# A selective-scan stack: VectorE takes delta*x for its own products from SBUF, without ScalarE's copy into PSUM

## The chip, the core and the metric

The kernel runs on one NeuronCore of a Trainium2 chip. The metric is the device time of one execution in microseconds (us), the median of several runs; before the change it is 22066.67 us, over three runs of 22064.29 to 22081.29 us. The core has a matrix engine (TensorE, PE in the profile), a vector engine (VectorE, DVE), an activation engine (ScalarE, ACT), a general engine (GpSimd, POOL) and an engine that issues the transfers (SyncE, SP). Each of them takes its own instructions in order. They wait for each other through semaphores. Two on-chip memories matter here: SBUF, the large one, and PSUM, the small one that TensorE writes its results into.

## What is computed

Four layers run over an input of 4 images, 64 x 64 positions, 128 channels. Layers 0, 1 and 3 are state-space blocks: normalisation, projection, a 3 x 3 convolution, four selective scans (by rows, by columns, and both of these backwards), a gate and a small network. Layer 2 is a gating layer. The scans are most of the work; cut to what matters:

```python
delta = softplus(dts + dt_b)
A = -exp(A_log).reshape(K, DI, N)                 # K = 4 scans, DI = 256 channels, N = 16 states

def step(h, t):
    x_t, d_t, B_t, C_t = t
    h = exp(d_t[..., None] * A) * h + (d_t * x_t)[..., None] * B_t[:, :, None, :]
    return h, einsum('bkdn,bkn->bkd', h, C_t)     # y: the sum over the 16 states
```

For each channel and each of 16 states this is a recurrence along 4096 positions with a decay `exp(delta*A)` and an input `(delta*x)*B`. `B` and `C` depend on the position and the state and not on the channel.

## The kernel before

The 4096 positions are cut into chunks of 512 (`CH`). A chunk belongs to one image, one layer and one of the four scans; there are 384 of them (12 turns of image and layer, 4 scans, 8 chunks). The 256 channels lie in two halves `m` of 128 partitions, the 16 states in four groups `q` of 4. A chunk is worked in 8 periods (`i`), one for each pair of group and half, so there are 3072 periods. Each period handles 4 states of 128 channels over 512 positions, in two sides of two states each:

- Side 0: the input is made by TensorE. `pair_db` multiplies the transposed delta*x with diagonal matrices of B (which ScalarE made in `diagonals`, line 891) into the PSUM tile `dbp` (line 899).
- Side 1: the input is made by VectorE. ScalarE's `lift` (line 916) copies one half of `s.du`, the product delta*x, from SBUF into a PSUM tile `dv`, at the end of the period before. Two products (lines 1048 and 1049) multiply it by the rows of B in `s.bb`. The first writes the other of two `dv` tiles, the second writes over its own input. Both have 128 x 512 elements, one operand in PSUM (`dv`) and one in SBUF (`bb`).

For each of the four states, ScalarE makes the decay `da` (line 908), VectorE runs the recurrence (`scan`, line 924) from `da` in SBUF and `dbp` or `dv` in PSUM into `h` in SBUF, and ScalarE saves the last element as the next chunk's initial state (`save`, line 932). GpSimd multiplies both states of a side by the rows of C, `cb` (`times_c`, line 936, 128 x 1024 elements), and in every second period adds the two sides (line 938). TensorE sums over the states by matmuls with the identity (line 951), and VectorE takes the sum out of PSUM (lines 962 and 964). GpSimd also makes `s.du` from delta and x, once per half and chunk (line 859). SyncE loads `bb` and `cb` as rows that are broadcast over the partitions (line 875).

The order on each engine is the order of the calls in the loop over `periods` (lines 985 to 1071); the program is scheduled by hand. In one period VectorE has: scan, scan (side 0), product, product, scan, scan (side 1). Everything else (normalisations, projections, convolutions, the small networks of the turns before and after) is cut into steps that `other` spreads over the periods, and the next chunk's preparation (`prologue`) comes in pieces by `piece`. The pools give `h` and `hc` four buffers each, `da` three, `du`, `bb` and `cb` two.

Of the kernel before, what the change touches and what calls it, by code (L numbers as in the profile page):

```python
# [13 lines left out]
F32 = mybir.dt.float32  # L14
# [11 lines left out]
CH = 512  # L26
NCH = L // CH
RPC = CH // W
P = 128
# [48 lines left out]
def cost(step):  # L78

    return getattr(step, "matmuls", 0) or (0.05 if step is empty else 0.25)  # L80
# [6 lines left out]
def alike(a, b):  # L87
    return empty in (a, b) or hasattr(a, "matmuls") == hasattr(b, "matmuls")


def when(place):

    chunk, place = divmod(place - 1, 4 * len(ROOM))
    i, number = divmod(place, 4)
    return chunk + (sum(ROOM[:i]) + ROOM[i] * number / 4) / sum(ROOM)
# [3 lines left out]
def vss_stack_kernel(ctx: ExitStack, tc: tile.TileContext, x: bass.AP, weights, out: bass.AP, n_batch=B, layers=(0, 1, 2, 3)):  # L99
# [6 lines left out]
    nc = tc.nc  # L106
# [660 lines left out]
    for turn, (e, i) in enumerate(turns):  # L767

        for nth, k in enumerate((1, 3, 0, 2) if turn else (0, 1, 3, 2)):
            for ci in range(NCH):  # L770
                s = SimpleNamespace(turn=turn, e=e, v=wt[i], layer=i, nth=nth, k=k, ci=ci)
# [17 lines left out]
    def meanwhile(turn):  # L789

        chunk, end = 4 * 8, 4 * 8 * (per_turn - 2) - 4
        if not turn:

            first = [(row, n * chunk, (n + 1) * chunk - 2) for n, row in enumerate(opening[4:])]
            rest = combine(1, psums), combine(3, psums), *between(turns[1][0], None, 0, psums)
            return first + spaced(rest, first[-1][2], end)
        rows = after(*turns[turn - 1])
        if turn + 1 == len(turns):

            last = [(row, n * chunk + 8, (n + 1) * chunk + 8) for n, row in enumerate(after(*turns[turn]), 3 * NCH + 1)]  # L800
            return spaced(rows, 8, last[0][1]) + last
        if turns[turn + 1][1] == 0:
            rows += between(turns[turn + 1][0], None, 0, psums)
        return spaced(rows, 8, end)
# [4 lines left out]
    def scans(pool, ring, deep, psum):  # L809
# [60 lines left out]
        def spread(s, q, b):  # L870

            rows_of, at, count = ((s.bb, CQ * q + 2, CQ - 2), (s.cb, CQ * q, CQ))[b]
            rows_of[q] = pool.tile([P, count, CH], F32, tag="bc"[b] + "b", name="bc"[b] + "b")
            row = R + b * N + at
            nc.sync.dma_start(
                out=rows_of[q], in_=s.xd_d[s.k // 2 : s.k // 2 + 1, row : row + count].to_broadcast([P, count, CH])
            )

        def place(s, i):


            q = i // 2
            return q, (i + q + s.flip) % 2
# [11 lines left out]
        def pair_db(s, i):  # L895
            q, m = place(s, i)
            s.db = psum.tile([P, CH, 2], F32, tag="dbp", name="dbp")
            for t in range(4):
                nc.tensor.matmul(  # L899
                    s.db[:, t * P : (t + 1) * P, :], s.duT[:, t, m, :], s.diag[q][:, t], start=True, stop=True  # L900
                )

        def decay(s, i, side):
            q, m = place(s, i)
            da = ring.tile([P, 2, CH], F32, tag="da", name="da")
            for j in range(2):
                n = CQ * q + 2 * side + j
                nc.scalar.activation(da[:, j], s.delta[:, m], AF.Exp, scale=s.v["a"][:, s.k, m, n : n + 1])  # L908
            return da

        dv = [psum.tile([P, CH], F32, name=f"dv{j}") for j in range(2)]

        def lift(s, i):
            nc.scalar.copy(dv[i % 2], s.du[:, place(s, i)[1]])  # L916

        def scan(s, i, side, j, da, db):
            q, m = place(s, i)
            if j == 0:  # L920
                s.h[i, side] = deep.tile([P, 2, CH], F32, tag="h", name="h")
            n = CQ * q + 2 * side + j
            init = 0.0 if s.first else s.state[:, m, n : n + 1]
            nc.vector.tensor_tensor_scan(  # L924
                s.h[i, side][:, j, s.step], da[:, j, s.step], db[:, s.step], init, ALU.mult, ALU.add
            )

        def save(s, i, side):
            if not s.last:
                q, m = place(s, i)  # L930
                n = CQ * q + 2 * side
                nc.scalar.copy(s.state[:, m, n : n + 2].unsqueeze(2), s.h[i, side][:, :, s.end : s.end + 1])  # L932

        def times_c(s, i, side):
            hc = s.hc[i, side] = deep.tile([P, 2, CH], F32, tag="hc", name="hc")
            nc.gpsimd.tensor_mul(hc, s.h[i, side], s.cb[i // 2][:, 2 * side : 2 * side + 2, :])  # L936
            if side == 1 and i in PAIRED:
                nc.gpsimd.tensor_add(hc, hc, s.hc[i, 0])  # L938
# [32 lines left out]
        s = chunks[0]  # L971
# [5 lines left out]
        spread(s, 0, 0)  # L977
        spread(s, 0, 1)
        pair_db(s, 0)
        lift(s, 0)  # L980
        da = [decay(s, 0, side) for side in range(2)]
        pro = None
        periods = [(s, i) for s in chunks for i in range(8)]
# [1 line left out]
        for at, (s, i) in enumerate(periods):  # L985
            then = periods[at + 1] if at + 1 < len(periods) else None
            if i == 0:
                nxt = chunks[at // 8 + 1] if at // 8 + 1 < len(chunks) else None
                if nxt:
                    pro, nxt.dt = prologue(nxt), s.dt  # L990
                s.state = pool.tile([P, 2, N], F32, tag="state", name="state") if s.first else before[0].state
                if at % (8 * per_turn) == 0:
                    segments = [
                        SimpleNamespace(todo=steps, done=0, dense=True, total=len(steps), frm=frm, to=to)

                        if to - frm <= 4 * 8
                        else SimpleNamespace(
                            todo=steps, done=0, dense=False, total=sum(map(cost, steps)), frm=when(frm), to=when(to)
                        )
                        for steps, frm, to in meanwhile(s.turn)  # L1000
                    ]

            def piece(number):

                if nxt and number in PIECES:
                    next(pro)

            def other(number):

                place = at % (8 * per_turn) * 4 + number  # L1010
                for g in segments:
                    gone = place if g.dense else when(place)
                    while g.todo and g.done < g.total * (gone - g.frm) / (g.to - g.frm):
                        step = g.todo.pop(0)
                        g.done += 1 if g.dense else cost(step)
                        step()

                        if gone < g.to and not g.dense and (step is empty or g.todo and not alike(step, g.todo[0])):
                            break

            da_next = [None, None]
            spreads = (s, i // 2 + 1) if i < 7 else (nxt, 0)
            if i % 2 == 0 or not spreads[0]:
                spreads = None
            if then:
                da_next[0] = decay(*then, 0)
            if before:
                save(*before, 1)
            if spreads:
                spread(*spreads, 0)  # L1030
            scan(s, i, 0, 0, da[0], s.db[:, :, 0])
            other(0)
            scan(s, i, 0, 1, da[0], s.db[:, :, 1])
            times_c(s, i, 0)

            if before and i % 2 == 0:
                add_up(*before, 0)
            if then:
                pair_db(*then)
            piece(2 * i)  # L1040
            other(1)
            if spreads:
                spread(*spreads, 1)
            if then:
                da_next[1] = decay(*then, 1)
            save(s, i, 0)
            du, db = dv[i % 2], dv[1 - i % 2]
            nc.vector.tensor_mul(db, du, s.bb[i // 2][:, 0])  # L1048
            nc.vector.tensor_mul(du, du, s.bb[i // 2][:, 1])  # L1049
            scan(s, i, 1, 0, da[1], db)  # L1050
            other(2)
            scan(s, i, 1, 1, da[1], du)
            times_c(s, i, 1)
            if then:
                lift(*then)

            q, half = (i + 2 + i % 2) // 2, 1 - i % 2
            if q < 4:
                diagonals(s, q, half)
            elif nxt:  # L1060
                diagonals(nxt, q - 4, half)
            if i < 2 and full:
                leave(*full.pop(0))
            if before:
                add_up(*before, *((2, 3) if i % 2 else (1, 2, 3)))
            piece(2 * i + 1)
            other(3)
            da = da_next
            before = (s, i)
            if then and then[0].turn != s.turn:  # L1070
                assert not any(g.todo for g in segments)
# [100 lines left out]
```

## Time and profile before

| what | value |
|---|---|
| median of the runs | 22066.67 us (22064.29 to 22081.29) |
| span of the profiled execution | 22070.4 us, 216982 instructions |
| one period (span / 3072) | 7.18 us |
| transfers, mean | 139 GB/s |
| mean granted TensorE clock | 0.963 |

The profile shows one execution. "Busy" is the time in which an engine worked on instructions, as a share of the span. A group of instructions is shown with its line, engine, operation, output and inputs, shapes, count, total busy time and mean duration, and behind the second bar the time for which the engine stood idle just before such instructions, with what ended most of that idle time. The times of two instructions on one engine can overlap by about a tenth of a microsecond, since the next one starts before the end of the one before is recorded; so the sum over groups is larger than the engine's busy time. TensorE's busy time is modelled and says little of how much it could still take.

### The profile page before, as it was taken

To read this page: it belongs to the slowest core of one execution; us is meant where nothing else is said; L and a number is where in the kernel's file an instruction comes from. 1 tells how busy PE (TensorE), PEld (TensorE's weight loads), DVE (VectorE), ACT (ScalarE), POOL (GpSimd) and SP (SyncE) were. 2 spreads that over 40 slices of the span, in tenths; PEclk is the share of its full clock that TensorE was granted. 3 is DMA by queue.
4 is the path that set the end of the run, shared out by engine and by line. 5 is a ranking of instruction groups with operands and counts; after the bars stand their busy time and mean duration, and the time that the engine had idled before them with its cause. 6 is when DMAs were issued, how large, how long until landed. Compare 5 with 4: busy or idle time off the path is not lost. (4 is left out here: it accounts for less than half of the span.)

```text
span 22070.4 us, 216982 instructions
## 1 busy us (share of the span) xinstructions
PE 19694.9 (89%) x58234; PEld 10511.8 (48%) x58234; DVE 19479.8 (88%) x20186; ACT 18587.9 (84%) x40022; POOL 19266.5 (87%) x8862
## 2 busy tenths in 40 slices
PE   7898998898889889889989988989988988898897
PEld 3444444444444444444444444444444444444443
DVE  5999999999888888899889899989988888889996
ACT  6888888888888888888888888888888888888887
POOL 5999899899888888888889888988988888889996
PEclk9999999999999999999999999999999999999999
DMA  4444444444335434434534544444443453354342
GB/s 109 147 149 146 135 144 149 136 139 151 130 131 139 142 128 140 146 133 145 144 138 144 145 141 140 141 147 134 142 149 127 137 143 137 131 140 145 140 144 101
DMA packets 2437559, 3060.10 MB, mean 139 GB/s; under 512 B 1753840, under 2 KB 1790064, under 8 KB 2238192
## 3 DMA queue, kind: packets, MB, share of 16 engines
q1 hardware_dynamic: 2436336, 3046.22, 44.4%
q8 instruction: 472, 7.73, 0.1%
q14 instruction: 751, 6.15, 0.1%
HBM read 2784.41 MB, written 261.49 MB: 138 GB/s over the span
## 5 line engine op out<-in xcount | busy, mean ns | idle before, releaser
L936 POOL TENSOR_TENSOR hc<-h,cb 128x1024 f32<-128x1024 f32 x6144 | 14399.4, 2363 | 2276.5 <-DVE h L924 1113.1
L951 PE MATMUL yp<-hc,ident 128*128 128x512 f32 x18432 | 9062.1, 618 | 688.3 <-POOL hc L938 546.8
L908 ACT ACTIVATE da<-delta,w 128x512 f32<-128x512 f32 x12288 | 8148.0, 713 | 543.5 <-DVE h L924 530.5
L924 DVE TENSOR_TENSOR_SCAN h<-da,state,dbp 128x512 f32<-128x512 f32 x5376 | 6573.3, 1262 | 818.9 <-PE dbp L899 576.0
L899 PE MATMUL dbp<-diag,duT 128*128 128x256 f32 x24576 | 6012.6, 388 | 652.4 <-DVE h L924 560.1
L924 DVE TENSOR_TENSOR_SCAN h<-da,state,dv 128x512 f32<-128x512 f32 x5376 | 6589.4, 1264 | 0.0
L899 PEld LDWEIGHTS dbp<-diag,duT 128*128 128x128 f32 x24576 | 4675.2, 193 | 2921.3 <-issue 1673.1
L951 PEld LDWEIGHTS yp<-hc,ident 128*128 128x128 f32 x18432 | 3483.6, 196 | 4999.1 <-issue 3656.8
L891 ACT ACTIVATE diag<-ident,bt 128x128 f32<-128x128 f32 x12288 | 3952.1, 402 | 0.0
L938 POOL TENSOR_TENSOR hc<-hc 128x1024 f32<-128x1024 f32 x1536 | 3624.1, 2359 | 120.4
L1048 DVE TENSOR_TENSOR dv<-dv,bb 128x512 f32<-128x512 f32 x3072 | 2088.3, 680 | 945.9 <-ACT dv L916 730.3
L916 ACT COPY dv<-du 128x512 f32<-128x512 f32 x3072 | 1799.1, 586 | 984.6 <-DVE h L924 977.1
L1049 DVE TENSOR_TENSOR dv<-dv,bb 128x512 f32<-128x512 f32 x3072 | 2118.4, 690 | 0.0
L444 PE MATMUL gap<-halo,cw 128*128 128x512 f32 x3456 | 1750.8, 604 | 5.9 <-DVE cen L281 2.2
L924 DVE TENSOR_TENSOR_SCAN h<-da,dbp 128x512 f32<-128x512 f32 x768 | 891.1, 1202 | 250.7 <-PE dbp L899 166.9
L859 POOL TENSOR_TENSOR du<-delta,xs 128x512 f32<-128x512 f32 x768 | 979.9, 1276 | 31.8 <-ACT delta L847 31.8
L842 PE MATMUL ps_dt<-xd,dt_w 8*128 8x512 f32 x1536 | 881.2, 654 | 130.2 <-ACT delta L845 78.2
L932 ACT COPY state<-h 128x2 f32<-128x2 f32 x5376 | 964.3, 179 | 0.0
L444 PEld LDWEIGHTS gap<-halo,cw 128*128 128x128 f32 x3456 | 628.1, 191 | 654.8 <-issue 617.8
L924 DVE TENSOR_TENSOR_SCAN h<-da,dv 128x512 f32<-128x512 f32 x768 | 893.8, 1204 | 0.0
L845 ACT ACTIVATE delta<-ps_dt,w 128x512 f32<-128x512 f32 x768 | 524.9, 683 | 103.0 <-PE ps_dt L842 98.2
L865 PEld LDWEIGHTS ps_duT<-ident,du 128*128 128x128 f32 x3072 | 383.7, 142 | 321.9 <-issue 255.8
(122 smaller groups left out, 11686.6 us busy)
## 6 DMA issues: line engine op xcount, KB each, us to landing
cb<-xd_d SPq DMA_DIRECT2D x1536, 1024.0 KB
bb<-xd_d SPq DMA_DIRECT2D x1536, 512.0 KB
xs<-x_row_d SPq DMA_DIRECT2D x192, 512.0 KB
xs<-x_col_d SPq DMA_DIRECT2D x192, 512.0 KB
x_col_d<-down SPq DMA_DIRECT2D x192, 256.0 KB
x_row_d<-wide SPq DMA_DIRECT2D x96, 512.0 KB
y_d<-y_sb SPq DMA_DIRECT2D x96, 512.0 KB
y<-y_d SPq DMA_DIRECT2D x96, 512.0 KB
```

What stands on the lines that cost most here:

```text
L444: nc.tensor.matmul(z.ps, z.cw[:, m, t, :], z.halo[c][:, dy : dy + RPC, dx : dx + W], start=(t == 0), stop=(t == 8),)
L859: nc.gpsimd.tensor_mul(s.du[:, m], s.delta[:, m], s.xs[:, m])
L891: nc.scalar.activation(s.diag[q][:, t, :, j], ident, AF.Copy, scale=s.bt[:, t, CQ * q + j : CQ * q + j + 1])
L899: nc.tensor.matmul(s.db[:, t * P : (t + 1) * P, :], s.duT[:, t, m, :], s.diag[q][:, t], start=True, stop=True)
L908: nc.scalar.activation(da[:, j], s.delta[:, m], AF.Exp, scale=s.v["a"][:, s.k, m, n : n + 1])
L916: nc.scalar.copy(dv[i % 2], s.du[:, place(s, i)[1]])
L924: nc.vector.tensor_tensor_scan(s.h[i, side][:, j, s.step], da[:, j, s.step], db[:, s.step], init, ALU.mult, ALU.add)
L936: nc.gpsimd.tensor_mul(hc, s.h[i, side], s.cb[i // 2][:, 2 * side : 2 * side + 2, :])
L938: nc.gpsimd.tensor_add(hc, hc, s.hc[i, 0])
L951: nc.tensor.matmul(getattr(s, f"yp{m}"), ident, s.hc[i, side][:, j], start=opens, stop=closes)
L1048: nc.vector.tensor_mul(db, du, s.bb[i // 2][:, 0])
L1049: nc.vector.tensor_mul(du, du, s.bb[i // 2][:, 1])
```

## The change

The two `dv` tiles of one PSUM bank each become one tile of two banks. `lift` goes, with its call ahead of the loop and its call in each period. The two products become one instruction of 128 x 1024 elements, which reads the half of `s.du` in SBUF twice over (a broadcast over the two states) and both rows of `s.bb` in SBUF, and writes both halves of `dv`. The scans of side 1 read those halves.

```diff
-        dv = [psum.tile([P, CH], F32, name=f"dv{j}") for j in range(2)]
-
-        def lift(s, i):
-            nc.scalar.copy(dv[i % 2], s.du[:, place(s, i)[1]])
+        dv = psum.tile([P, 2, CH], F32, name="dv")
...
         pair_db(s, 0)
-        lift(s, 0)
         da = [decay(s, 0, side) for side in range(2)]
...
             save(s, i, 0)
-            du, db = dv[i % 2], dv[1 - i % 2]
-            nc.vector.tensor_mul(db, du, s.bb[i // 2][:, 0])
-            nc.vector.tensor_mul(du, du, s.bb[i // 2][:, 1])
-            scan(s, i, 1, 0, da[1], db)
+            du = s.du[:, place(s, i)[1] : place(s, i)[1] + 1]
+            nc.vector.tensor_mul(dv, du.to_broadcast([P, 2, CH]), s.bb[i // 2])
+            scan(s, i, 1, 0, da[1], dv[:, 0])
             other(2)
-            scan(s, i, 1, 1, da[1], du)
+            scan(s, i, 1, 1, da[1], dv[:, 1])
             times_c(s, i, 1)
-            if then:
-                lift(*then)
```

## The prediction

> **What bounds the kernel now.** I read the busy times first:
>
> ```profile
> span 22070.4 us, 216982 instructions
> ...
> PE 19694.9 (89%) x58234; PEld 10511.8 (48%) x58234; DVE 19479.8 (88%) x20186; ACT 18587.9 (84%) x40022; POOL 19266.5 (87%) x8862
> ```
>
> No engine stands out. Over 3072 periods of 7.18 us (22070.4 / 3072) this is 6.34 us of VectorE, 6.27 of GpSimd, 6.05 of ScalarE. VectorE has 0.84 us of idle time in a period and GpSimd 0.91. An addition of half a microsecond to one of them can hide in idle time only in part, because that idle time is waiting for the others. The groups around the change, from the list of costly groups, come next:
>
> ```profile
> L936 POOL TENSOR_TENSOR hc<-h,cb 128x1024 f32<-128x1024 f32 x6144 | 14399.4, 2363 | 2276.5 <-DVE h L924 1113.1
> ...
> L1048 DVE TENSOR_TENSOR dv<-dv,bb 128x512 f32<-128x512 f32 x3072 | 2088.3, 680 | 945.9 <-ACT dv L916 730.3
> L916 ACT COPY dv<-du 128x512 f32<-128x512 f32 x3072 | 1799.1, 586 | 984.6 <-DVE h L924 977.1
> L1049 DVE TENSOR_TENSOR dv<-dv,bb 128x512 f32<-128x512 f32 x3072 | 2118.4, 690 | 0.0
> ```
>
> The reader is to see a ring. ScalarE's copy waits 977.1 us in all for VectorE's last scan, which still reads the `dv` tile; VectorE's first product waits 730.3 us for the copy. The wait table says how often, and what else VectorE waits for:
>
> ```profile
> DVE h L924 <- PE dbp L899: 742.8, 557, 8.6
> DVE dv L1048 <- ACT dv L916: 730.3, 328, 7.5
> DVE dv L1048 <- DMA bb<-xd_d: 196.1, 64, 6.3
> ```
>
> So only 328 of 3072 products wait for the copy, by 2.2 us each: in most periods the copy is early. The timeline shows one quiet period, and the pitch of VectorE's instructions (columns: start, duration, engine, line):
>
> ```profile
> 11017.59 0.68 DVE L1048 TENSOR_TENSOR dv<-dv,bb 128x512 f32<-128x512 f32 x1
> ...
> 11018.17 0.69 DVE L1049 TENSOR_TENSOR dv<-dv,bb 128x512 f32<-128x512 f32 x1
> ...
> 11018.77 2.44 DVE L924 TENSOR_TENSOR_SCAN h<-da,state,dv 128x512 f32<-128x512 f32 x2
> ```
>
> The two products hold VectorE for 11018.77 - 11017.59 = 1.18 us, not for 0.68 + 0.69. Last, the spread of GpSimd's product from the view of its line, and the one VectorE product of 1024 elements from the groups kept apart by shape:
>
> ```profile
> L936 POOL TENSOR_TENSOR hc<-h,cb x6144: 2329/2362/2415, 167.9 to 21988.9; 128x1024 f32<-128x1024 f32 x199
> ```
>
> ```profile
> L379 DVE TENSOR_TENSOR y<-y,gap 128x1024 f32<-128x1024 f32 x96 | 115.3, 1201 | 39.9 <-PE gap L376 39.9
> ```
>
> GpSimd's 6144 products take 2329 to 2415 ns (minimum, maximum), whatever VectorE does beside them. All frequent VectorE rows of today have at most one wide operand in SBUF: the scans read `da` there and `dbp` or `dv` in PSUM, the products read `bb` there and `dv` in PSUM. So the trace shows that such instructions and GpSimd's do not disturb each other. It shows nothing of a VectorE instruction with two wide SBUF operands beside a GpSimd one; `du` with `bb` would be the first.
>
> **What goes.** The copy: 3072 x 0.586 us = 1799 us of ScalarE, 0.59 us a period, and the 0.32 us a period (977.1 / 3072) that ScalarE stands in front of it. ScalarE is not the bound, so this counts only through what it lets VectorE do: the wait of 730.3 / 3072 = 0.24 us a period. What stands next after it: the wait for TensorE's `dbp` (742.8 us), which needs ScalarE's diagonals, queued directly behind the copy; these come earlier too. No new wait arises in the program: the product waits for `bb` and for VectorE's own last scan, as before. SyncE and GpSimd issue the same instructions in the same order, the transfers too. `du` is held one period longer, but its two buffers are filled a whole chunk apart, so nothing is queued behind that.
>
> **What merges.** One product of 1024 elements takes 1.20 us by the row of line 379 (also with an operand that is broadcast over two halves), and if its tail overlaps by the same 0.10 us as today (0.68 against a pitch of 0.58) it holds VectorE for 1.10 us instead of 1.18: 0.08 us a period. VectorE's work is then 6.34 - 0.08 = 6.26 us, its other idle time 0.84 - 0.24 = 0.60 us.
>
> **What the second SBUF operand costs.** GpSimd is busy 87% of the time, so nearly each product meets a GpSimd instruction that reads two SBUF operands. The bounds for VectorE: nothing, if the pair behaves as all pairs of today do; or a whole GpSimd instruction, 2.36 us, if the product must let one pass. I exclude a gain, since one more operand to fetch from SBUF speeds nothing up. For GpSimd: nothing, or the whole 1.20 us for which the product runs. I take the middle for VectorE, half of 2.36 us times 0.87, or 1.03 us a period: the row nearest in what it reads is GpSimd's own product, the only frequent row with two wide SBUF operands, and it takes 2.36 us for what VectorE does in 1.20, so I don't take the free end.
>
> The Trainium skill, page "SBUF — State Buffer", section "Who interferes with whom", speaks against the change. It says that a VectorE instruction with two SBUF inputs contends with a GpSimd instruction that reads SBUF, its second input coming through a read interface that both use, and it calls the contention an exclusive lock. By this rule GpSimd would also stand for the whole product, 6.27 + 1.20 + 0.55 = 8.02 us a period or 24,640 us; by the undisturbed row of line 936 alone the time would be the 21,600 us of the second rival below. No run so far shows which holds for this pair.
>
> **The sum.** VectorE in a period: 6.26 + 1.03, and of its 0.60 us of other waits I keep three quarters, 0.45, because GpSimd and TensorE gain time to get ahead while VectorE is held: 7.74 us. Times 3072 this is 23,780, say 23,800 us, 7.8% over the span of 22070.4 us. That span is within 4 us of the median of the runs, so the same number stands for the median. GpSimd must fit in too: held by half a product it has 6.27 + 0.60 = 6.87, and with the part of its idle time that is not waiting for scans (0.91 - 1113.1/3072 = 0.55) 7.42 us, less than 7.74; held by a whole product 8.02 us, or 24,640. So VectorE sets the end in the middle case and GpSimd in the worst plausible one.
>
> **The rivals.** First, the two share smoothly: reads interleave and each loses about half a product. VectorE: 6.26 + 0.60 + 0.45 = 7.31 us; GpSimd 7.42 us, which decides: 22,800 us. For it speaks that neither can be reading in each nanosecond (GpSimd takes 2.36 us for 2 x 1024 elements); against it nothing in the trace.
>
> Second, on the other side: no contention at all. Then VectorE loses the wait and the 0.08 us, up to 0.32 us a period, 6.86 us or 21,090 us. I would expect half of it, since the waits for `dbp`, `bb` and the side work (0.60 us) come up next and GpSimd needs 6.27 us in any case: 7.02 us, 21,600 us. For it speaks the narrow spread of GpSimd's rows; against it that no pair of that kind is among them. It decides while the product's extra time and GpSimd's stay under about 0.3 us together; above this the change costs more than the copy's wait gave. An operand broadcast on VectorE is no obstacle, by line 379, and the program shows one product per period and no copy, so that the change does what it says is not in doubt.
>
> Third, VectorE loses each time: the product lets a whole GpSimd instruction pass, 2.36 us: 6.26 + 2.36 + 0.45 = 9.07 us, 27,860 us. Against it: scans late by so much leave GpSimd idle (only four `h` buffers), and an idle GpSimd holds nobody up.
>
> **How the numbers follow.** My chances: the forecast 0.48, smooth sharing 0.30, no contention 0.15, VectorE always last 0.07. The predicted time is the forecast's, 23,800 us. The range reaches from 22,400 us (under the sharing case, whose half product may be less) to 25,200 us (over the 24,640 of the fully held GpSimd); what is left out is the contention-free case and most of the third rival. The likeliest case's own range is 23,300 (only half of the other waits left, 7.59 us) to 24,640 us. A change of under 0.2%, 44 us, can't be told from none here. Faster is the second rival but for a sliver, 0.14; within 0.2% is that sliver and the mildest sharing, 0.03; slower 0.83.
>
> **What would show it.** Right: the merged product's mean well over 1.2 us with a wide spread (from 1.2 to 3.5 us), GpSimd's line 936 no longer within 2329 to 2415 ns, ScalarE's busy time lower by some 1800 us with its freed time idle. Product near 2.2 us and GpSimd's untouched would mean that VectorE alone pays; product at 1.2 and GpSimd's mean up by 0.4 us or more would mean that GpSimd pays, and the end is then set by it. Wrong: both rows as today and the wait of 730 us gone, with a span near 21,600 us. If GpSimd's group keeps its mean and its idle time grows, the third rival is the one.

## The result, and the profile after

The changed kernel takes 24045.27 us (median of four runs, 24038.53 to 24060.6) against 22065.48 us before (22061.73 to 22081.29): 1.0898 times as long, 95% interval 1.0882 to 1.0913. The forecast was 23,800 us. The profiled execution has a span of 24038.6 us, 7.82 us a period.

The head of its page, and the costly groups that answer to those shown of before (line 1044 is the merged product, 933 and 935 GpSimd's product with C and its addition, 859 its delta*x):

```profile
span 24038.6 us, 207966 instructions
...
PE 20275.4 (84%) x58234; PEld 10629.6 (44%) x58234; DVE 22169.1 (92%) x17114; ACT 17166.7 (71%) x36950; POOL 21971.8 (91%) x8862
...
L933 POOL TENSOR_TENSOR hc<-h,cb 128x1024 f32<-128x1024 f32 x6144 | 16035.1, 2627 | 1681.8 <-DVE h L921 888.0
...
L921 DVE TENSOR_TENSOR_SCAN h<-da,state,dv 128x512 f32<-128x512 f32 x5376 | 6611.5, 1268 | 365.5 <-ACT da L908 9.8
L1044 DVE TENSOR_TENSOR dv<-du,bb 128x1024 f32<-128x1024 f32 x3072 | 6383.8, 2078 | 176.9 <-DMA bb<-xd_d 176.6
...
L935 POOL TENSOR_TENSOR hc<-hc 128x1024 f32<-128x1024 f32 x1536 | 4335.1, 2822 | 120.4
...
L859 POOL TENSOR_TENSOR du<-delta,xs 128x512 f32<-128x512 f32 x768 | 1294.7, 1686 | 33.3 <-ACT delta L847 33.3
```

ScalarE is relieved (84% to 71%), and VectorE and GpSimd, which do less and the same as before, are both busier: 92% from 88, and 91% from 87. Their instructions have become longer. The product takes 2078 ns, not the 1.20 us of an equally long one; GpSimd's three groups went from 2363, 2359 and 1276 ns to 2627, 2822 and 1686. The wait does not appear as idle time. It lies inside the recorded durations, so only a group's mean and spread show it. The views of the two lines give the spread (minimum, median, maximum in ns):

```profile
L1044 DVE TENSOR_TENSOR dv<-du,bb x3072: 1195/2001/3454, 166.5 to 23955.9; 128x1024 f32<-128x1024 f32 x192
```

```profile
L933 POOL TENSOR_TENSOR hc<-h,cb x6144: 2329/2362/3454, 166.6 to 23960.3; 128x1024 f32<-128x1024 f32 x199
```

GpSimd's minimum is that of before (2329), the product's is about the 1201 ns of line 379. The maximum of both is 3454 = 2362 + 1092 ns: a whole GpSimd instruction and all but the first 0.12 us of a product (1.209 us, below), end to end. The timeline of the two engines shows how it comes about (start, duration, engine, line):

```profile
11012.30 2.35 POOL L935 TENSOR_TENSOR hc<-hc 128x1024 f32<-128x1024 f32 x1
11013.17 2.57 DVE L1044 TENSOR_TENSOR dv<-du,bb 128x1024 f32<-128x1024 f32 x1
...
11014.73 3.22 POOL L933 TENSOR_TENSOR hc<-h,cb 128x1024 f32<-128x1024 f32 x1
11015.84 2.45 DVE L921 TENSOR_TENSOR_SCAN h<-da,state,dv 128x512 f32<-128x512 f32 x2
```

The addition on GpSimd ends at 11014.65. The product was recorded as started at 11013.17, but ends at 11015.74, 1.09 us after the addition. GpSimd's next instruction is recorded from 11014.73 and takes 3.22 us: 0.86 us longer than alone, for it must let the product finish. Over all records of the trace, 2757 of 3072 products start while a GpSimd instruction runs, and 2629 are longer than 1.3 us. Of these, 99 in 100 end between 1.086 and 1.096 us after the end of that GpSimd instruction. The 315 products that find GpSimd free take 1.209 us in the mean. The other way round, 2544 of GpSimd's products with C and additions start inside a product of VectorE, and 99 in 100 of them end between 2.19 and 2.23 us after it. So these instructions of the two engines exclude each other as wholes; the records show no sharing within them.

### The profile page after: what moved, and what is told of

Its sections match the earlier page's. It is cut to its first block, busy times and chain, and to the rows that moved or that the text cites. A ratio compares the mean times of both kernels' runs of the same rounds, so it can differ in the third digit from the quotient of the medians.

```text
span 24038.6 us, 207966 instructions
## 1 busy us (share of the span) xinstructions
PE 20275.4 (84%) x58234; PEld 10629.6 (44%) x58234; DVE 22169.1 (92%) x17114; ACT 17166.7 (71%) x36950; POOL 21971.8 (91%) x8862
## 5 line engine op out<-in xcount | busy, mean ns | idle before, releaser
L933 POOL TENSOR_TENSOR hc<-h,cb 128x1024 f32<-128x1024 f32 x6144 | 16035.1, 2627 | 1681.8 <-DVE h L921 888.0
L948 PE MATMUL yp<-hc,ident 128*128 128x512 f32 x18432 | 9399.4, 636 | 1741.3 <-POOL hc L935 1370.3
L899 PE MATMUL dbp<-diag,duT 128*128 128x256 f32 x24576 | 6126.8, 394 | 1120.4 <-DVE h L921 1086.0
L921 DVE TENSOR_TENSOR_SCAN h<-da,state,dv 128x512 f32<-128x512 f32 x5376 | 6611.5, 1268 | 365.5 <-ACT da L908 9.8
L1044 DVE TENSOR_TENSOR dv<-du,bb 128x1024 f32<-128x1024 f32 x3072 | 6383.8, 2078 | 176.9 <-DMA bb<-xd_d 176.6
L899 PEld LDWEIGHTS dbp<-diag,duT 128*128 128x128 f32 x24576 | 4725.2, 196 | 3497.2 <-issue 2327.8
L935 POOL TENSOR_TENSOR hc<-hc 128x1024 f32<-128x1024 f32 x1536 | 4335.1, 2822 | 120.4
L859 POOL TENSOR_TENSOR du<-delta,xs 128x512 f32<-128x512 f32 x768 | 1294.7, 1686 | 33.3 <-ACT delta L847 33.3
L921 DVE TENSOR_TENSOR_SCAN h<-da,dv 128x512 f32<-128x512 f32 x768 | 897.3, 1208 | 52.2 <-POOL du L859 1.1
L867 ACT COPY duT<-ps_duT 128x512 f32<-128x512 f32 x768 | 445.6, 580 | 421.0 <-PE ps_duT L865 418.3
L269 ACT ACTIVATE sq<-cen 128x512 f32<-128x512 f32 x256 | 161.3, 630 | 519.8 <-DVE cen L265 380.5
L961 DVE TENSOR_TENSOR y_sb<-y_sb,yp 128x512 f32<-128x512 f32 x576 | 508.3, 882 | 4.6 <-PE yp L948 3.8
```

What stands on the lines that cost most here:

```text
L859: nc.gpsimd.tensor_mul(s.du[:, m], s.delta[:, m], s.xs[:, m])
L899: nc.tensor.matmul(s.db[:, t * P : (t + 1) * P, :], s.duT[:, t, m, :], s.diag[q][:, t], start=True, stop=True)
L921: nc.vector.tensor_tensor_scan(s.h[i, side][:, j, s.step], da[:, j, s.step], db[:, s.step], init, ALU.mult, ALU.add)
L948: nc.tensor.matmul(getattr(s, f"yp{m}"), ident, s.hc[i, side][:, j], start=opens, stop=closes)
L1044: nc.vector.tensor_mul(dv, du.to_broadcast([P, 2, CH]), s.bb[i // 2])
```

## The experiments

Theory A in the expectations is this exclusion. Theory B is the rival that the merged product and the missing copy of ScalarE bring the loss by themselves. Times of before in the comparisons were 22,052 to 22,059 us.

**One wide operand instead of two.** The product with delta*x is left out. The place, the size and the count of the instruction stay; the operation is another one, a product with one number per partition.

```diff
-            nc.vector.tensor_mul(dv, du.to_broadcast([P, 2, CH]), s.bb[i // 2])
+            nc.vector.tensor_scalar_mul(dv, s.bb[i // 2], s.v["dsum"][:, 0:1])
```

> The changed kernel, but its merged product multiplies the two rows of B by one number per partition: it reads one wide operand from SBUF instead of two and is otherwise as long and as placed. The product with delta*x is left out. Theory A (the second wide SBUF operand makes VectorE and GpSimd exclude each other for whole instructions): the product's mean falls from 2.08 to about 1.2 us, GpSimd's product with C is back at 2.33 to 2.42 us throughout, and the time is 21,500 to 22,000 us, at or below that of the kernel before. Theory B (the merging and the missing copy lengthen the chain, since the scan now stands directly behind a product of 1024 elements): the time stays above 23,000 us.

Measured: 22,026.6 us, 0.999 times before (0.998 to 0.9999), 27 us above the expected range of 21,500 to 22,000. Its groups and the view of line 933:

```profile
L933 POOL TENSOR_TENSOR hc<-h,cb 128x1024 f32<-128x1024 f32 x6144 | 14404.8, 2363 | 2243.3 <-DVE h L921 1089.1 <-DMA cb<-xd_d 358.9 <-issue 254.1
...
L1043 DVE TENSOR_SCALAR dv<-bb,dsum 128x1024 f32<-128x1024 f32 x3072 | 3884.9, 1265 | 258.2 <-DMA bb<-xd_d 258.1
```

```profile
L933 POOL TENSOR_TENSOR hc<-h,cb x6144: 2332/2362/2418, 166.9 to 21939.4; 128x1024 f32<-128x1024 f32 x199
```

With the second SBUF operand gone, GpSimd's rows are as narrow as before the change and 2,019 us of the 24,045 are gone. That is the whole loss. Theory B falls. But next to nothing is gained against the kernel before either, and the next runs ask why. A part of it is this run's own: its product takes 1265 ns and not the 1209 of a free product of the changed kernel, at most 172 us over 3072 periods (an estimate).

**The merging alone**, with ScalarE's copy and the operand in PSUM. The states come in the order in which the second may overwrite the input:

```diff
...
-            nc.vector.tensor_mul(db, du, s.bb[i // 2][:, 0])
-            nc.vector.tensor_mul(du, du, s.bb[i // 2][:, 1])
+            du, db = dv[:, i % 2], dv[:, 1 - i % 2]
+            both = dv if i % 2 else dv[:, ::-1]
+            nc.vector.tensor_mul(both, du.unsqueeze(1).to_broadcast([P, 2, CH]), s.bb[i // 2])
```

> The kernel before with its ScalarE copy into PSUM, but with its two products merged into one of 128 x 1024 elements, which reads delta*x from PSUM. Only the merging is tested. Theory A: no long product and no long GpSimd instruction; the merged product and the gap behind it hold VectorE for 1.32 us where the pair held it for 1.18, at most 0.14 us a period, so 22,066 to 22,500 us. Theory B: most of the loss is here, above 23,000 us.

Measured: 22,448.08 us, 1.0177 (1.0162 to 1.0192), as theory A had it. Here the operation and its size are those of the changed kernel, and only one operand lies in SBUF. Neither engine's row is stretched:

```profile
L1049 DVE TENSOR_TENSOR dv<-dv,bb x3072: 1194/1208/1244, 166.6 to 22366.4; 128x1024 f32<-128x1024 f32 x192
```

```profile
L936 POOL TENSOR_TENSOR hc<-h,cb x6144: 2331/2363/2420, 166.8 to 22370.3; 128x1024 f32<-128x1024 f32 x199
```

VectorE's timeline shows what the merging costs:

```profile
11007.34 1.21 DVE L1049 TENSOR_TENSOR dv<-dv,bb 128x1024 f32<-128x1024 f32 x1
...
11008.65 2.45 DVE L924 TENSOR_TENSOR_SCAN h<-da,state,dv 128x512 f32<-128x512 f32 x2
```

The scan starts 0.10 us after the product's end, since it waits for what the product just wrote. Before the change, the first scan read the first of two products, and each of those was overlapped by its successor by 0.09 us. From start to start the median is 1.312 us here, against 0.582 + 0.597 before: 0.133 us x 3072 = 409 us, of which 394 were measured.

**The product in two instructions**, each with two SBUF operands:

```diff
-            nc.vector.tensor_mul(dv, du.to_broadcast([P, 2, CH]), s.bb[i // 2])
+            for j in range(2):
+                nc.vector.tensor_mul(dv[:, j], du[:, 0], s.bb[i // 2][:, j])
```

> The changed kernel with its product in two instructions of 128 x 512 elements, each with two wide SBUF operands. Theory A: if GpSimd takes its turn between the two, the second waits for a whole GpSimd instruction of 2.36 us, its mean goes to 2 to 3 us and the time to 26,000 us or more; if VectorE keeps its turn, the second is 0.69 us and the time 23,500 to 24,000 us. Theory B (merging is the loss): about 0.2 us a period faster than the changed kernel, 23,400 us. If the two engines shared by element, both products would be about 1.0 us and the time as that of the changed kernel.

Measured: 28,691.02 us, 1.301 (1.2991 to 1.3029). The timeline of the two engines (x2 marks two merged neighbours):

```profile
11022.26 5.11 POOL L933 TENSOR_TENSOR hc<-h,cb 128x1024 f32<-128x1024 f32 x2
11022.48 5.45 DVE L1045 TENSOR_TENSOR dv<-du,bb 128x512 f32<-128x512 f32 x2
```

GpSimd takes its turn between the two products. In this stretch each of them waits for a GpSimd instruction, and two of those and both products fill 5.67 us, from 11022.26 to 11027.93. Of the 6144 products 4535 are longer than 0.8 us (2910 of the 3072 second ones, 1625 of the first), and 98 in 100 of these end 0.553 to 0.561 us after the GpSimd instruction. The mean of all 6144 is 1956 ns, that of those which find GpSimd free 0.68 us. Merging helps here: with two operands in SBUF it saves 4,646 us, with one in PSUM it costs 394.

Why GpSimd gets in between is not settled by this run. In the trace each second product waits for a semaphore that the end of the first one sets, and it starts 34 to 35 ns after that end; both write the tile `dv`. Line 1049 of the kernel before has no such wait and starts 0.09 us before the end of line 1048. So when the first product ends, the second is not ready at once, and a waiting GpSimd instruction is. Two products without a wait between them were not run.

**GpSimd in halves**, on the changed kernel and, as control, on the one before:

```diff
-            nc.gpsimd.tensor_mul(hc, s.h[i, side], s.cb[i // 2][:, 2 * side : 2 * side + 2, :])
+            for j in range(2):
+                nc.gpsimd.tensor_mul(hc[:, j], s.h[i, side][:, j], s.cb[i // 2][:, 2 * side + j, :])
```

> The changed kernel with GpSimd's product with C in two instructions of 128 x 512 elements (1.27 us each) for one of 1024 (2.36 us). If the product waits for the end of the running GpSimd instruction, its mean falls (the wait of 0.88 us goes to 0.45 to 0.6 us, so 1.65 to 1.8 us; the longest beside these halves 1.09 + 1.27 = 2.4 us, though the additions of 1024 still stand) while GpSimd's own work grows by 0.38 us a period. Against its own control (next run) the loss should be 4 to 7% instead of 9%. If the engines shared by element, the product's mean would stay at 2.08 us.

> The control for the run with GpSimd's halves: the kernel before with the same halves. GpSimd has 6144 x (2 x 1.275 - 2.363) = 1,150 us more work, 0.37 us a period, of which its idle time of 0.91 us can take a part: 22,300 to 23,000 us, with both engines' rows as narrow as in the kernel before.

Measured: 24,011.34 us (1.0891, 1.0875 to 1.0907) and the control 22,192.57 us (1.0067, 1.0052 to 1.0082). Between the two that is 8.2%, not 4 to 7%, and the control lies below its expected 22,300 to 23,000: both expectations missed. The groups of the changed kernel with halves:

```profile
L934 POOL TENSOR_TENSOR hc<-h,cb 128x512 f32<-128x512 f32 x12288 | 17312.1, 1440 | 708.2 <-DVE h L921 329.7 <-DMA cb<-xd_d 253.9 <-PE yp L949 20.9
...
L1045 DVE TENSOR_TENSOR dv<-du,bb 128x1024 f32<-128x1024 f32 x3072 | 5799.1, 1888 | 166.6 <-DMA bb<-xd_d 166.4
```

The product is shorter, by 0.19 us and not the expected 0.28 to 0.43, which still speaks against sharing by element. But GpSimd pays as before: (1440 - 1274) x 12288, (2657 - 2359) x 1536 and (1624 - 1275) x 768 ns, 2,766 us or 0.90 us a period. With its halves that brings it to 95% busy, and VectorE's wait for GpSimd (`hc`) goes from 32.5 to 164.3 us, that for `dbp` from 568.1 to 920.0; GpSimd seems to be the bound now. A shorter GpSimd instruction shortened what VectorE waits, not what GpSimd waits.

**Which of the two decides?** Half of GpSimd's additions go to TensorE, on both kernels:

```diff
-PAIRED = (0, 2, 4, 6)
+PAIRED = (0, 4)
...
-            if before and i % 2 == 0:
+            if before and before[1] not in PAIRED:
                 add_up(*before, 0)
...
-                add_up(*before, *((2, 3) if i % 2 else (1, 2, 3)))
+                add_up(*before, *((2, 3) if before[1] in PAIRED else (1, 2, 3)))
```

> The changed kernel with half of GpSimd's additions of the two sides (line 935) given to TensorE, which sums all four states of those periods itself: 768 GpSimd instructions less (0.59 us a period at their old 2.36 us), 1536 matmuls more (0.31 us a period at 0.62 us). It asks which engine sets the end in the changed kernel. If it is GpSimd, held by the products: 1,000 us or more faster than the changed kernel, under 23,050 us. If it is VectorE, waiting for GpSimd's instructions: GpSimd is less often busy when a product comes, so the product's mean falls, but only by about a tenth (0.59 of 7.15 us of GpSimd's work), 0.1 us a period, 23,700 us or so.

> Its control: the kernel before with the same half of the additions given to TensorE. Neither engine is held by the other there, so the trade is 0.59 us of GpSimd against 0.31 us of TensorE in a period in which both have 0.8 to 0.9 us of idle time: 21,800 to 22,400 us. Under 21,900 us it would beat both kernels.

Measured: 23,699.69 us (1.0745, 1.0727 to 1.0763) and the control 22,326.97 us (1.0127, 1.0111 to 1.0142). The control loses, with VectorE's wait for `dbp` at 1,214.7 us instead of 742.8, so TensorE has little to spare; the changed kernel gains 346 us nevertheless. Its busy line:

```profile
PE 21084.9 (89%) x61306; PEld 11145.4 (47%) x61306; DVE 21578.6 (91%) x17114; ACT 17166.0 (72%) x36950; POOL 19970.1 (84%) x8094
```

GpSimd went from 91% to 84% and VectorE from 92% to 91%. The product fell to 1.879 us. The time is the 23,700 us of the branch in which VectorE decides, but by itself it includes TensorE's added work. Against the control the difference is 346 + 268 = 614 us, and the product's shortening is (2.078 - 1.879) x 3072 = 611 us; GpSimd's busy time fell by 2,002 us. So the time followed VectorE's product and not GpSimd's work.

**What the copy was worth.** Two runs. First as the one-operand run, in two instructions:

```diff
+            for j in range(2):
+                nc.vector.tensor_scalar_mul(dv[:, j], s.bb[i // 2][:, j], s.v["dsum"][:, 0:1])
```

> As the one-operand experiment, but in two instructions of 128 x 512 elements: no ScalarE copy, no merging, no second SBUF operand; the product with delta*x is left out. It prices the copy alone. By the second rival's working the copy's wait of 0.24 us a period is worth half to all of itself: 21,330 to 21,700 us. From the runs before it, the merging cost 394 us and the one-operand kernel came out 28 us under the kernel before, so the copy should be worth about 420 us or some more: 21,450 to 21,650 us. If the wait is only passed on to TensorE's products or to the transfers, 21,950 us or more.

Measured: 22,390.53 us (1.015, 1.0133 to 1.0167), a miss. The comparison was bad: a pair holds VectorE for 1.65 us in the median (in one period from 11000.51 to 11002.16), against 1.18. Of the 0.47 us more, some 0.12 are the form, which takes 743 ns and not 680 to 690. The rest is lost overlap: here too the second product waits for the first, and the scan for the second. The better run leaves out seven of eight copies and keeps VectorE's instructions:

```diff
-            if then:
+            if then and i == 7:
                 lift(*then)
```

> The kernel before with seven of eight of ScalarE's copies left out: the products go on from what the last ones left in PSUM, so the result is not the reference's, but VectorE's instructions are those of the kernel before, one for one. It prices the copy without the longer products that the two one-operand kernels had. If VectorE's wait for the copy (730 us) comes back in full, 7/8 of it: 22,054 - 640, about 21,400 us. If only half (as the second rival assumed), 21,700 us. If the wait passes to others, 22,000 us.

Measured: 21,816.9 us, 0.9894 (0.9877 to 0.991): 235 us for seven eighths of the copies, in proportion 268 us for all (an estimate), between the expected 21,700 and 22,000. The wait table of this run, against before:

```profile
DVE h L924 <- PE dbp L899: 972.1, 659, 8.1
DVE dv L1048 <- DMA bb<-xd_d: 239.7, 70, 7.6
DVE cen L265 <- PE gap L261: 163.2, 68, 32.2
DVE h L924 <- ACT da L908: 148.6, 121, 16.9
```

VectorE's wait for the copy is down from 730.3 to 61.9 us, but `dbp` went from 742.8 to 972.1, `bb` from 196.1 to 239.7, the decays from 104.7 to 148.6. Of the 668 us that went, 235 came back as time; 317 are found again in these three waits.

The prices do not add up. 394 us for the merging less 268 for the copy would put the one-operand run 126 us above the kernel before; it lies 28 below. So behind a merged product the missing copy is worth more, 422 us between these two runs. Why is open.

**Three other ways.** The copy behind the four diagonals (`lift` called after `diagonals`):

> The kernel before, with ScalarE's copy placed behind the four diagonals of its period instead of ahead of them. It asks what ScalarE's standing ahead of the copy (977 us) and VectorE's wait for it (730 us) are worth without a second SBUF operand. If ScalarE's standing is what delays the diagonals and with them the whole ring: ScalarE's wait for VectorE ahead of the copy nearly gone, and 21,600 to 21,950 us. If the copy now comes too late for the product: VectorE's wait for it grows above 730 us and the time is 22,066 us or more.

Measured: 22,115.69 us, 1.0029 (1.0017 to 1.004). ScalarE's wait ahead of the copy fell from 977.1 to 50.4 us, but VectorE's wait for the copy rose:

```profile
DVE dv L1048 <- ACT dv L916: 1118.3, 481, 8.1
```

The second branch of the expectation holds. VectorE's wait for the copy rose by 388 us and the time by only 62, while its wait for `dbp` fell from 742.8 to 642.7 us and that for `bb` from 196.1 to 136.3: a part was given back there, through the earlier diagonals as it seems, and the later copy cost more. The merged product from PSUM, between the two scans of side 0:

> The merged product from PSUM, placed between the two scans of side 0, so that a scan which does not read it stands directly behind it. If the loss of the merged kernel (1.8%) is the gap between the product's end and the scan that reads it, the gap goes, the product holds VectorE for 1.10 us, and the time is 21,800 to 22,000 us. If the copy now comes too late for a product that stands 1.2 us earlier, VectorE's wait for it grows from 814 us to 1,200 us or more and the time stays near 22,100 us or above.

Measured: 22,948.22 us, 1.0403 (1.0388 to 1.0419). The gap is gone (the next scan, which does not read the product, starts 1.12 us after its start, 0.09 us before its end), but VectorE waits 1,453.9 us for the copy and 1,082.9 us for `dbp`, each more than before. And delta*x brought in by TensorE:

```diff
-            nc.scalar.copy(dv[i % 2], s.du[:, place(s, i)[1]])
+            nc.tensor.matmul(dv[i % 2], ident, s.du[:, place(s, i)[1]], start=True, stop=True)
```

> The kernel before, with delta*x brought into PSUM by TensorE (a matmul with the identity) and not by ScalarE: the one other way here to get rid of ScalarE's copy without a second SBUF operand. TensorE gets 3072 matmuls of 128x512 more, 0.62 us each by the row of the sums over the states, 1,900 us in all. If TensorE has that much to spare (its busy time is modelled), 21,500 to 21,950 us; if it is itself near its limit, 22,500 us or more, with longer waits of VectorE for TensorE's products.

Measured: 22,861.82 us, 1.0365 (1.035 to 1.0381), with TensorE 95% busy and VectorE waiting 1,372.0 us for `dbp`. No version that computes the whole beats the kernel before.

## Why the prediction was right, point by point

**The second SBUF operand.** This was the step that decided, and its middle value was near: 1.03 us a period on VectorE (half a GpSimd instruction, 87% of the time), measured 2.078 - 1.20 = 0.88. That both engines pay, and VectorE sets the end, holds. The mechanism was not worked out: half a GpSimd instruction stood there as the middle of two bounds, with GpSimd's own slow row as the reason. What the trace shows is a wait to the end of the running instruction, 0.97 us in the mean for the 2757 products that met one. That such a wait comes out near half an instruction is partly luck of the middle. The Trainium skill's rule ("SBUF — State Buffer", "Who interferes with whom": an exclusive lock for two SBUF inputs against GpSimd's reads) agrees with the 1.09 us between the end of the one and the end of the other. The 24,640 us that I worked out from it were too high, as they held GpSimd for a whole product of 1.20 us in each period, where 0.87 us were measured.

**What GpSimd pays.** I left it between nothing and 1.20 us and put half, 0.60, into the sum. Measured is the sum of the three groups' longer times, (16035.1 - 14399.4) + (4335.1 - 3624.1) + (1294.7 - 979.9) = 2,662 us, 0.87 us a period: 2910 of the 8448 instructions of these groups are longer, by 0.92 us in the mean. By the prediction's own sum GpSimd needs 6.27 + 0.87 + 0.55 = 7.69 us, a little under the measured 7.82, so the end was still VectorE's, as the forecast said; the run with fewer additions speaks for that.

**The merging.** Wrong in sign. "If its tail overlaps by the same 0.10 us as today" failed: the instruction behind it reads what it wrote and starts 0.10 us after it instead of 0.10 us before. The step was put at a gain of 0.08 us and costs 0.13 in the run with the merging alone.

**The copy.** All of the 0.24 us was taken off VectorE's idle time; alone it is worth 268 / 3072 = 0.09 us. The ring was read slightly wrong: the scan that ScalarE's copy waits for is not VectorE's last one but the first of side 1, which reads the tile that the copy overwrites; in the trace 983.0 of the 984.6 us of idle time ahead of the copy end with that scan. ScalarE's busy time fell by 1,421 us, not some 1800: its instructions overlap too.

**The remaining idle time.** I kept 0.45 us; measured is (24038.6 - 22169.1) / 3072 = 0.61 us, of which 0.14 is the gap ahead of the side-1 scans ((365.5 + 52.2) / 3072), 0.47 without it.

**The sum.** 6.26 + 1.03 + 0.45 = 7.74 became 6.26 + 0.88 + 0.08 (lost overlap) + 0.14 (gap) + 0.47 = 7.83 us, the measured 7.82. This is a division of the measured period into busy and idle time, not a price of each step by itself. A product too dear by 0.15 and a merging too cheap by 0.22 us nearly cancelled; that the total came so near is luck.

**The rivals.** Smooth sharing fell with the ends 1.09 us after GpSimd's. The third rival, a whole GpSimd instruction each time, is nearly what the second of two separate products met (2910 of 3072 long, 2.69 us in the mean), at 28,691 us. The contention-free case was put at 21,600 us; without a second SBUF operand the changed kernel takes 22,027. Its price was off by the two steps above, the merging and the copy, and by the 1265 ns of that run's product. With that taken off (at most 172 us, an estimate) this change would, even without contention, have gained 1% at most.

## What to carry to other kernels

Before moving an operand of a VectorE instruction into SBUF, count its wide SBUF operands and look at how busy GpSimd is: with two, VectorE here waited out the running GpSimd instruction and GpSimd waited out the product, and neither wait showed as idle time. A copy into PSUM by an engine with time to spare can be the cheaper price, here 268 us against some 2,000. Where two SBUF operands can't be avoided, one long instruction was better here than two short ones of which the second waits for the first, as GpSimd took its turn between them.

## What the runs showed of the hardware that was not expected

Two VectorE products, the second held back to 34 or 35 ns after the first, did not keep the turn: between two products of 0.68 us GpSimd got in with an instruction of 2.36 us in 2910 of 3072 pairs. Whether the hold-back or the order of the requests decides is open. The exclusion is also exact: 1.086 to 1.096 us from the end of one to the end of the other, where a free product takes 1.209 us, so a waiting product seems to have some 0.12 us of its start behind it when its turn comes (an estimate from the two).
